# Making the one-hots of an edge-attention kernel on POOL (GpSimd) instead of DVE (VectorE)

## The chip, the cores and the metric

The kernel runs on one core of a Trainium2 chip. Its time is that of one execution on the device, in microseconds; the median of several runs is compared. Engines are named as the profile names them: PE is TensorE's matrix multiplication and PEld its weight load, DVE is VectorE, ACT is ScalarE, POOL is GpSimd and SP is SyncE. POOL here issues the indirect DMAs that gather rows by a list of indices; SP issues the plain loads and stores.

## The reference

One layer of a graph network with attention by edge type: N = 3125 nodes, E = 100000 edges sorted by their destination, R = 5 edge types, 8 heads of 16 channels (H = 128). For every destination and type there is a softmax of its own over the incoming edges.

```python
out = zeros(n, 8, 16)
for r in range(5):
    mask = edge_types == r
    q = einsum('eh,khd->ekd', x[dst], W_Q[r]); k = einsum('eh,khd->ekd', x[src], W_K[r])
    v = einsum('eh,khd->ekd', x[src], W_V[r])
    logits = (q * k).sum(-1) / 4 + attn_bias[r]
    max_v = segment_max(where(mask, logits, -1e9), dst)
    exp_l = where(mask, exp(logits - max_v[dst]), 0)
    attn = exp_l / (segment_sum(exp_l, dst)[dst] + 1e-12)
    out += segment_sum(attn[:, :, None] * v, dst)
out = out.reshape(n, 128) @ out_proj_w.T + out_proj_b
h = layernorm(out + x) * ln_gamma + ln_beta
return layernorm(x + h)
```

## The kernel before

A preparatory phase of about 90 us projects all nodes by all types into a table in HBM, `kv_d` (a row of 256 float32, key and value, for every node and type), and makes `key_d`: for every group of 512 edges the number 5 x (destination - first destination of the group) + type, in bf16. Queries are written, a block of nodes at a time and through the whole run, to `q_d` in three bf16 parts.

Then one loop runs over steps. A group is 512 edges (4 tiles of 128), there are 196 groups, and each step does the *first pass* of one group and the *second pass* of a group 16 to 19 earlier (the maxima of a node must be known before its second pass), 215 steps in all. A block of nodes is finished about every eight steps.

First pass of group g, in the order in which its parts happen:

- `fetch_keys` and `fetch_q` (L365 to L373): SP loads the keys, the same row to all partitions, as `kt` (128 KB, three buffers), and a window of queries as `qw`. This is done three steps ahead.
- `gather` (L678 to L681): POOL issues four indirect DMAs, each of 128 rows of 1 KB, from `kv_d` into one of 21 buffers. A buffer is free when `weigh` of the group 21 earlier is done. Nine groups are gathered before the loop; in the loop a gather is issued two steps ahead.
- `spot` (L735 to L738): the one-hot `hot`, 125 rows by 512 edges in bf16, is 1 where the edge's key is the row's number: one comparison of `kt` with a scalar per partition, `row_of`. It has 21 buffers and is used twice. It is issued two steps ahead, and is the last of the regular instructions of its step on DVE.
- `spread_q` (L740 to L749): PE multiplies the one-hot with the three parts of the queries, 12 matmuls, so that every edge has its query in `qe`. One step ahead.
- `logits` (L756 to L762): DVE multiplies keys and queries (`prod`, L759) and sums by head (L760) into `lg`; SP stores it (L765).

Once per block of nodes, `maxima_load` (L770) collects the block's logits with one indirect DMA on POOL (`ell`, L772), and `maxima` (L779 to L831, DVE) finds the maxima in pieces spread over several steps.

Second pass: `spread_m` (L857, PE) spreads the maxima with the same one-hot, its last use; `less_max` (L872, DVE), `exps` (L876, ACT), `weigh` (L881, DVE: `wv`), `places` (L901 and L904, ACT: `at`), `sums` (L907 to L925, PE: `pp`), `carry` (ACT), `norm` (L936 to L939, DVE: `den`, `o`) and, per block, the projection, the residual and both norms.

The order on each engine is that in which the loop's body is written; no scheduler moves anything. The part that matters here:

```python
        if v is not None:
            weigh(v)
        while gathered < NGR - 1 and step_of[gathered + 1] <= k + AHEAD:   # AHEAD = 2
            gathered += 1
            gather(gathered)
        ...                        # maxima_load, less_max, exps, weights, types, norm
        if g is not None:
            logits(g)
            store_logits(g)
        if k + 2 in group_at:
            spot(group_at[k + 2])
```

Of the kernel before, what the change touches and what calls it, by code (L numbers as in the profile page):

```python
# [12 lines left out]
ALU = mybir.AluOpType  # L13
# [33 lines left out]
WR = WN * R  # L47
# [85 lines left out]
def windowed_path(  # L133
# [4 lines left out]
    nc = tc.nc  # L138
# [90 lines left out]
    def iota(name, pattern, n, base=0, mult=0, dt=F32, pool=const):  # L229
        t = pool.tile([P, n], dt, name=name)  # L230
        nc.gpsimd.iota(
            t, pattern=pattern, base=base, channel_multiplier=mult,
            allow_small_or_imprecise_dtypes=True,
        )
        return t

    node = iota("node", [[P, NT]], NT, mult=1)
    row_of = iota("row_of", [[0, 1]], 1, mult=1)
# [113 lines left out]
    live = {}  # L352
# [381 lines left out]

    def spot(g):  # L735
        hot = hold.tile([WR, T, P], BF16, name="hot")
        nc.vector.tensor_scalar(hot, live.pop(("kt", g))[:WR], row_of[:WR], None, op0=ALU.is_equal)  # L737
        live["hot", g] = hot  # L738

    def spread_q(g):  # L740
# [321 lines left out]
    for k in range(-2, root_at[NT] + 2):  # L1062
        v, g = v_at.get(k), group_at.get(k)
# [59 lines left out]
        if k + 2 in group_at:  # L1123
            spot(group_at[k + 2])
# [535 lines left out]
```

## Time and profile before

| | |
|---|---|
| time, median of 3 runs | 1592.43 us (1591.39 to 1598.67) |
| time of the profiled execution | 1586.14 us |
| its span | 1584.3 us |
| mean granted TensorE clock | 0.714 |
| one-hots on DVE (L737) | 196, 69.2 us busy, 354 ns each |
| gathers on POOL (L681) | 784, 746.9 us busy, 953 ns each |
| maxima loads on POOL (L772) | 25, 23.7 us busy |
| moved by DMA | 203.63 MB |

The profile is of one execution, so sums over its rows are made against 1586.14 us and not against the median. Busy times count only work: the issue of plain DMAs, semaphores and register instructions are left out, but POOL's indirect DMAs are counted, with the time for which POOL is held. In a row of a group, the number behind the bar is busy time in us and the mean of one in ns; then comes the idle time of the engine just before these instructions and what ended most of it.

### The profile page before, as it was taken

How to read it: one execution, taken by the hardware profiler on the slowest of the kernel's cores; microseconds unless marked ns; L12 is line 12 of the kernel's file. 1: busy time of each engine (PE TensorE's matmuls, PEld its weight loads, DVE VectorE, ACT ScalarE, POOL GpSimd, SP SyncE). 2: the span in 40 equal slices, each digit the busy share in tenths (PEclk: the TensorE clock that was granted, in tenths of full speed). 3: DMA queues.
4: the chain of work that ended last, by engine and by line, in shares of the span. 5: the costliest groups of instructions: out<-in, count | busy, mean ns of one | idle time of the engine just before them, and what ended most of it. 6: DMA issues, size and time to landing. Idle time of an engine off the chain costs nothing.

```text
span 1584.3 us, 25675 instructions
## 1 busy us (share of the span) xinstructions
PE 966.0 (61%) x7526; PEld 746.3 (47%) x7526; DVE 928.1 (59%) x2559; ACT 632.1 (40%) x2248; POOL 801.8 (51%) x901
## 2 busy tenths in 40 slices
PE   7940424666666666666556567666666665656775
PEld 3520322545555544545445445454454544545564
DVE  4530722665666466556647646646656665665686
ACT  2630122344444443444434444444444344444354
POOL 2556445445555465455555555555546555555500
PEclk9965556666776687677877777668767677766687
DMA  6963634444554454454554555445445445454400
GB/s 173 362 207 100 149 95 127 118 114 113 137 135 119 127 134 123 116 139 117 129 134 116 134 142 118 120 128 134 121 125 137 123 125 134 115 132 123 115 16 15
DMA packets 180889, 203.63 MB, mean 129 GB/s; under 512 B 83207, under 2 KB 146083, under 8 KB 180620
## 3 DMA queue, kind: packets, MB, share of 16 engines
q0 software_dynamic: 40896, 113.39, 24.8%
q1 hardware_dynamic: 135414, 83.80, 22.9%
q10 hardware_dynamic: 4430, 4.71, 1.1%
q8 instruction: 63, 1.03, 0.3%
q14 instruction: 86, 0.70, 0.1%
HBM read 166.50 MB, written 35.28 MB: 127 GB/s over the span
## 4 chain that ended last, share of the span: by engine, by line
issue 27%; DVE 26%; PE 24%; another core or an unknown queue 7%; ACT 6%; DMA 5%; POOL 3%; SPq 2%; DVEq 0%; ACTq 0%
PE pp L915 8%; DVE prod L759 4%; DVE lg L760 4%; DVE wl L810 4%; DVE wv L881 3%; PE me L863 3%; PE qe L746 3%; PE pr L395 3%; POOL kv L681 3%; DMA mw<-m_d 2%; ACT at L901 2%; DVE mx L816 2%; PE pp L917 2%; DVE hot L737 1%
## 5 line engine op out<-in xcount | busy, mean ns | idle before, releaser
L681 POOL DMA_INDIRECT kv<-kv_d,idx x784 | 746.9, 953 | 602.0 <-DVE den L936 316.4
L915 PE MATMUL pp<-wv,at 128*125 128x136 f32 x1568 | 395.5, 385 | 55.8 <-issue 53.1
L915 PEld LDWEIGHTS pp<-wv,at 128*125 128x125 f32 x1568 | 297.4, 256 | 125.5 <-issue 121.4
L746 PE MATMUL qe<-qw,hot 125*128 125x128 bf16 x2352 | 226.9, 259 | 115.8 <-DVE lg L760 48.6
L863 PE MATMUL me<-mw,hot 125*128 125x64 bf16 (+1 forms) x2352 | 142.2, 218 | 213.7 <-issue 93.0
L746 PEld LDWEIGHTS <-hot 125*128 125x128 bf16 x2352 | 203.5, 126 | 128.7 <-issue 68.7
L876 ACT ACTIVATE me<-me 128x32 f32<-128x32 f32 x196 | 35.7, 182 | 555.9 <-DVE me L872 340.6
L872 DVE TENSOR_TENSOR me<-lg,me 128x32 f32<-128x32 f32 x196 | 37.7, 192 | 373.5 <-remote 170.8
L863 PEld LDWEIGHTS <-hot 125*128 125x128 bf16 x2352 | 125.8, 114 | 249.8 <-issue 213.9
L901 ACT ACTIVATE at<-row_at,nkey 128x125 f32<-128x125 f32 x744 | 237.6, 398 | 0.0
L881 DVE TENSOR_TENSOR wv<-kv,me 128x512 f32<-128x512 f32 x196 | 132.9, 678 | 86.6 <-remote 70.1
L759 DVE TENSOR_TENSOR prod<-kv,qe 128x512 f32<-128x512 f32 x196 | 132.9, 678 | 70.8 <-remote 31.2
L917 PE MATMUL pp<-pt,carried 125*5 125x136 f32 x390 | 100.2, 348 | 63.2 <-ACT pt L930 35.4
L760 DVE TENSOR_REDUCE lg<-prod 128x32 f32<-128x512 f32 x196 | 134.5, 686 | 6.8
L904 ACT ACTIVATE at<-at 128x500 f32<-128x500 f32 (+1 forms) x196 | 117.3, 599 | 6.2
L707 PE MATMUL prq<-wq,xTq 128*128 128x384 f32 (+1 forms) x88 | 51.7, 676 | 108.1 <-DVE hot L737 56.7
L924 PEld LDWEIGHTS pp<-rsum,o 125*128 125x128 f32 x392 | 83.3, 255 | 28.1 <-issue 28.0
L924 PE MATMUL pp<-rsum,o 125*128 125x25 f32 x392 | 74.1, 268 | 24.6 <-issue 20.7
L810 DVE TENSOR_TENSOR wl<-by_head,shut 128x1024 f32<-128x1024 f32 (+2 forms) x73 | 76.9, 1053 | 12.9 <-ACT by_head L787 7.5
L816 DVE TENSOR_REDUCE mx<-wl 128x16 f32<-128x1024 f32 (+2 forms) x73 | 76.5, 1048 | 2.5
L707 PEld LDWEIGHTS prq<-wq,xTq 128*128 128x128 f32 x88 | 19.6, 273 | 116.0 <-DVE hot L737 59.6
L949 ACT COPY oT<-pp 128x25 f32 x196 | 33.2, 169 | 99.1 <-remote 62.3
(184 smaller groups left out, 1024.7 us busy)
## 6 DMA issues: line engine op xcount, KB each, us to landing
kt<-key_d SPq DMA_DIRECT2D x196, 128.0 KB
qw<-q_d SPq DMA_DIRECT2D x196, 96.0 KB
kv_d<-kvs SPq DMA_DIRECT2D x24, 640.0 KB
kv<-kv_d,idx POOLq DMA_INDIRECT x784
q_d<-q SPq DMA_DIRECT2D x22, 480.0 KB
lg_d<-lg SPq DMA_DIRECT2D x196, 18.0 KB
mw<-m_d SPq DMA_DIRECT2D x196, 6.0 KB
xr<-in_x SPq DMA_DIRECT2D x24, 64.0 KB
```

The lines of the kernel that those rows point to most:

```text
L681: nc.gpsimd.indirect_dma_start(out=kv[:, t, :], out_offset=None, in_=kv_d[:, :], in_offset=bass.IndirectOffsetOnAxis(ap=idx[:, t, g : g + ...
L746: nc.tensor.matmul(qe[:, t, :], hot[:, t, :], qw[:WR, s, :], start=(s == 0), stop=(s == 2))
L759: nc.vector.tensor_tensor(prod, kv[:, :, :H], live.pop(("qe", g)), op=ALU.mult)
L760: nc.vector.tensor_reduce(lg[:, :, :HEADS], prod.rearrange("p t (k d) -> p t k d", d=HD), AX.X, ALU.add)
L810: nc.vector.tensor_tensor(wl, by_head[:, None].to_broadcast([P, n, nh, D]), shut[:, :n, None, :].to_broadcast([P, n, nh, D]), op=ALU.add,)
L863: nc.tensor.matmul(me[:, t], hot[:, t, :], mw[:WR, None, :, s, :].to_broadcast([WR, times, 2, HEADS // 2]), start=(s == 0), stop=(s == 2),)
L881: nc.vector.tensor_tensor(wv[:, :, :H].rearrange("p t (k d) -> p t k d", d=HD), kv[:, :, H:].rearrange("p t (k d) -> p t k d", d=HD), live ...
L901: nc.scalar.activation(at[:, t, :], row_at[:, :WR], AF.Abs, bias=nkey[:, t, g : g + 1], scale=1.0)
L904: nc.scalar.activation(at[:, on_dve:], at[:, on_dve:], AF.Relu, bias=1.0, scale=-1.0)
L915: nc.tensor.matmul(pp, at[:, t, :], wv[:, t, :], start=(t == 0), stop=(t == T - 1))
L917: nc.tensor.matmul(pp[:R], carried[:WR, g, :], live.pop(("pt", g - 1)), start=False, stop=False,)
L924: nc.tensor.matmul(op, live.pop(("o5", done)), rsum[:WR], start=True, stop=True)
```

## The change

The comparison that makes the one-hot is issued on POOL instead of DVE, except for the first two groups, which stay on DVE. The call stays where it was in the loop, behind the gathers of the same step, so that on POOL each one-hot stands directly behind the four gathers of its own group (behind the maxima load too, in the steps that have one). The one-hots of groups 2 to 8 stand behind the nine groups gathered ahead of the loop.

```diff
     def spot(g):
         hot = hold.tile([WR, T, P], BF16, name="hot")
-        nc.vector.tensor_scalar(hot, live.pop(("kt", g))[:WR], row_of[:WR], None, op0=ALU.is_equal)
+        on = nc.vector if g < 2 else nc.gpsimd
+        on.tensor_scalar(hot, live.pop(("kt", g))[:WR], row_of[:WR], None, op0=ALU.is_equal)
         live["hot", g] = hot
```

The load of the keys of a later group into the same buffer of `kt` (SP) now waits for POOL instead of DVE, and so does the first weight load of `spread_q` on PE. The orders of instructions on PE, ACT and SP are unchanged.

## The prediction

> **What bounds the kernel now.** I read the busy shares first, then the chain that ended last, the groups, the waits, and windows of the steady loop. All sums are made against the profiled execution (1586.14 us: span 1584.3 and 1.84 outside it); the median of the three timed runs, 1592.43 us, lies 6.3 us above it, and I add that at the end.
>
> Busy shares and the chain:
>
> ```profile
> PE 966.0 (61%) x7526; PEld 746.3 (47%) x7526; DVE 928.1 (59%) x2559; ACT 632.1 (40%) x2248; POOL 801.8 (51%) x901
> issue 27%; DVE 26%; PE 24%; another core or an unknown queue 7%; ACT 6%; DMA 5%; POOL 3%; SPq 2%; DVEq 0%; ACTq 0%
> PE pp L915 8%; DVE prod L759 4%; DVE lg L760 4%; DVE wl L810 4%; DVE wv L881 3%; PE me L863 3%; PE qe L746 3%; PE pr L395 3%; POOL kv L681 3%; DMA mw<-m_d 2%; ACT at L901 2%; DVE mx L816 2%; PE pp L917 2%; DVE hot L737 1%
> ```
>
> No engine is full, and the largest share of the chain, 27%, is "issue": an engine that waited for nothing the profile shows. The one-hot has 1% of the chain. The groups of the change, the engine it leaves and the engine it goes to:
>
> ```profile
> L737 DVE TENSOR_SCALAR hot<-kt,row_of 125x512 bf16<-125x512 bf16 x196 | 69.2, 354 | 4.0 <-DMA kt<-key_d 3.1 <-DMA q_d<-q3s 0.9
> L681 POOL DMA_INDIRECT kv<-kv_d,idx x784 | 746.9, 953 | 602.0 <-DVE den L936 316.4 <-issue 213.1 <-DVE me L872 15.8
> L772 POOL DMA_INDIRECT ell<-lg_d,start_i x25 | 23.7, 949 | 60.4 <-DMA kt<-key_d 24.7 <-DVE me L872 19.1 <-DVE wl L810 7.4
> ```
>
> The waits before a gather, by what ended them (sum in us, count, longest):
>
> ```profile
> POOL kv L681 <- DVE den L936: 316.4, 71, 10.0
> POOL kv L681 <- issue: 213.1, 676, 1.2
> ```
>
> A gather is 0.95 us, and before 676 of the 784 POOL waits for nothing but 213.1 / 676 = 0.3 us of issue, so a group of four holds POOL 4 x (0.95 + 0.30) = 5.0 us. The multiplication `prod` (L759) of group 40 starts at 406.9 us and that of group 190 at 1478.5: 7.14 us per step. With one maxima load of 1.25 us per eight steps POOL needs 5.17 us of a step, and a block of eight steps (57.1 us) has 57.1 - 41.3 = 15.8 us in which POOL waits. The step is thus longer than POOL's 5.17 and than DVE's 4.43 (its busy time of those steps). Where does the rest go? Windows, two of the fill (no pauses between gathers, then no gathers) and two of one steady block:
>
> ```profile
> core 0: us, PE busy (x) PEld busy (x) DVE busy (x) ACT busy (x) POOL busy (x), PEclk, DMA share, GB/s
> 125.00:154.00 29.00, 0.16 (x2) 0.00 (x0) 0.00 (x0) 0.00 (x0) 19.93 (x21) 0.50 0.38 105
> 154.00:177.00 23.00, 13.26 (x113) 10.37 (x113) 17.64 (x34) 2.62 (x11) 0.95 (x1) 0.63 0.50 97
> 755.60:774.30 18.70, 6.88 (x63) 5.09 (x63) 5.51 (x14) 7.67 (x23) 12.33 (x13) 0.75 0.56 161
> 779.20:797.50 18.30, 10.76 (x106) 8.23 (x103) 17.18 (x43) 9.51 (x36) 11.37 (x12) 0.86 0.52 129
> ```
>
> ```profile
> 764.41 0.95 POOL L681 DMA_INDIRECT kv<-kv_d,idx  x1 [0.31 <-issue]
> ...
> 770.68 0.95 POOL L681 DMA_INDIRECT kv<-kv_d,idx  x1 [0.30 <-issue]
> 779.20 0.95 POOL L681 DMA_INDIRECT kv<-kv_d,idx  x1 [7.57 <-DVE den L936]
> ...
> 785.59 0.95 POOL L681 DMA_INDIRECT kv<-kv_d,idx  x1 [1.68 <-DVE den L936]
> ...
> 791.22 0.95 POOL L681 DMA_INDIRECT kv<-kv_d,idx  x1 [0.93 <-issue]
> ```
>
> In 755.6 to 774.3 three groups and a maxima load leave POOL with no pause, and DVE works 5.5 of 18.7 us; in 779.2 to 797.5 three groups with pauses of 1.68 and 0.93 us between them stand beside 17.2 busy us of DVE in 18.3. The fill shows it bare: 29 us of 21 gathers, and PE, DVE and ACT at rest. I counted this over groups 40 to 189: the 51 that start within 0.4 us of the one before have DVE busy 10% of their time, the 62 behind a pause of 0.4 to 3 us 82%, the 37 behind a longer one 85%. I read it so: while gathers run on without a pause, the other engines' instructions crawl. It isn't proved, since the pattern repeats identically in every block: the steps with pauses are those with maxima (much DVE work at hand), and the runs follow quick steps. The readings "runs starve the rest" and "the rest has nothing to do in a run" part at the quick steps.
>
> **The change, part by part.** DVE loses 194 one-hots x 0.354 us = 68.7 us. Most of that lies beside other work: the chain gives `hot` 1%, about 16 us, and this is the gain if nothing else moves. Two one-hots stay on DVE. PE's, ACT's and SP's orders are unchanged.
>
> POOL gains 194 instructions. In its order the nine groups gathered ahead of the loop come first, then the one-hots of groups 2 to 8, then four gathers and a one-hot for each further group (behind the maxima load where there is one).
>
> *Price of a one-hot on POOL.* The trace has no such operation. Nearest are the set-up rows: an iota takes 0.122 us for one element, 0.175 for 64 and 0.233 for 128 (0.9 ns for each further element), and the affine select, which reads and writes 128 elements, 0.293, which over the same 0.12 fixed is 1.35 ns per element. For 512 elements this gives 0.12 + 0.46 = 0.58 us by the iota and 0.12 + 0.69 = 0.81 by the affine select; I take the second, for it has an input. The upper end is twice that, 1.6 us, as a scalar per partition and bf16 are in no POOL row. With 0.30 between instructions h = 1.1 us, ends 0.9 and 1.9.
>
> The Trainium skill ("GPSIMD Engine Reference", elementwise side by side) speaks against this change: it calls GpSimd the wrong engine for ordinary elementwise work, Vector being roughly twice as fast, and its best of about 1.8 cycles per element would make, as an estimate, 0.77 us here. By that page the change is a loss on each instruction; the DVE row of 0.354 agrees with the direction, and whether POOL's idle time pays for it is not a matter the page decides.
>
> *POOL's pace* becomes 5.17 + 1.1 = 6.3 us (6.1 to 7.1) against steps of 7.14. Break-even is h = 1.97.
>
> *A pause in each run.* A group now has 1.1 us without a gather behind it, as long as the pauses of 0.93 to 1.68 beside which DVE was 82% busy. If these end the crawl, the quick steps (2.9 us of DVE work) proceed under the gathers and POOL sets the pace: a block is 8 x (5.0 + 1.1) + 1.25 = 50.1 us. I leave it 1.3 us of waits for buffers (the 21 buffers even out the blocks' long steps of 5.6 to 6.4 us), so 51.4 against 57.1: 5.7 less, over 165 steps or 20.6 blocks, 117 us. With h = 0.9 a block is 49.8 (150 us less), with h = 1.6 it is 55.4 (35 less), with 1.9 some 57.8: nothing gained.
>
> *New waits.* A one-hot on POOL waits for its keys (`kt`) and for its buffer of 21 (freed by PE's `spread_m`). Behind it stand all later gathers. Keys are loaded three steps ahead, 128 KB, and the 4.0 us of idle before L737 are the only trace of them being late, so I take nothing. SP's load of the next keys now waits for POOL, and behind that stand SP's other loads and the stores of logits; as POOL stands a step ahead, nothing is late. PE's `spread_q` needs the one-hot one step later, but it is queued behind four gathers. In the profile `spread_q` starts on average 2.64 us after the gathers of its group end, yet in about a quarter of the steps up to 1.6 us before it. Those steps would wait: some 0.6 us per step on average if the pace were unchanged. In the likely case a faster PE waits for POOL anyway, and this is in the pace.
>
> *The fill.* Today the first run of gathers lasts to 151 us; it will end at 136, when the one-hots wait for keys. PE, DVE and SP start up to 15 us earlier, and the gathers of 9 to 20 come at 6.1 us each instead: I take half, 7 us.
>
> The sum: 1586 - 117 - 7 = 1462 on the profiled execution, and 1468 on the median. As h has more room above 1.1 than below, and 1.3 us of waits a block is sparing (now it is 15.8), I put the likeliest at 1485, with 1430 to 1565 as its own range (h of 0.9, and h of 1.7 with 16 us from DVE).
>
> **The rivals.** (1) *The rest still crawls and POOL is only longer* (slower). If the stall is not ended by a one-hot behind a group, or comes from the order of the work and not from the gathers, then POOL's 15.8 us of waits per block stay and 8 x 1.1 = 8.8 us are added: 20.6 x 8.8 = 181 us, 1773 on the median. If only the quarter of the steps in which `spread_q` waits for the one-hot is paid, it is 0.6 x 165 = 100 us: 1692. For it: cause and occasion coincide in every block, and POOL waits mostly for `den`, the end of `weigh` of a slow step. Against it: the pauses of 0.93 us did suffice. It decides once h plus the waits that stay go above 1.97 us a step. (2) *Hidden and worth nothing*: POOL's 15.8 idle us a block take the 8.8, and the 68.7 us of DVE were not on the path: 1592, or 1576 with the chain's 16 us. That the change does not do what it says is no rival: the two built programs differ by these 194 instructions and the waits that go with them, and by nothing else.
>
> **How the numbers follow.** Likely case 0.55, the slower rival 0.35, the neutral one 0.10. A measurement of this kernel tells about 0.5% (8 us) from no change; half of the neutral case falls within that, the other half, with the chain's 16 us, is faster, and of the likely case 0.01 ends within 0.5% (h near 1.9). Faster 0.59, same 0.06, slower 0.35. The range runs from 1430 (h = 0.9) to 1690 (the waits of `spread_q` paid in full), which leaves out some 0.05 below and 0.15 above. The likeliest case alone would be 1430 to 1565.
>
> **What would show it.** Right: a POOL one-hot of 0.6 to 1.1 us, no stretch of 10 us with DVE under 30%, POOL over 80% busy with its gaps, "issue" well below 27% of the chain, idle time of L681 behind `den` falling from 316 to under 100 us. Wrong: one-hots of over 1.6 us, PE rows of L746 that wait for `hot` on POOL, or windows behind the one-hot in which DVE is still at rest; then the crawl isn't ended by a pause of this length, or wasn't made by the runs.

## The result, and the profile after

The changed kernel took 1506.32 us (median of 4 runs, 1504.7 to 1506.73) beside 1593.89 us for the kernel before in the same comparison: a ratio of 0.9445, 95% interval 0.9421 to 0.947. Its profiled execution took 1506.07 us, with a span of 1504.3, against 1586.14 and 1584.3 before. The prediction said 1485 in 1430 to 1690. As the experiments show further down, the sign of this result goes with the chip it ran on: on another chip the same change made the kernel 21% slower.

The page of the changed kernel: busy shares, the two lines of the chain that ended last, and three groups (busy us, mean ns, then idle before and what ended most of it):

```profile
PE 1005.8 (67%) x7526; PEld 800.1 (53%) x7526; DVE 901.7 (60%) x2365; ACT 637.9 (42%) x2248; POOL 1123.9 (75%) x1095
POOL 36%; PE 26%; issue 15%; DVE 11%; DMA 7%; another core or an unknown queue 2%; SPq 1%; ACT 1%; DVEq 0%; POOLq 0%; ACTq 0%
POOL kv L681 22%; POOL hot L738 14%; PE qe L747 6%; PE pp L916 6%; PE me L864 5%; DMA kv<-kv_d,idx 5%; PE pr L395 3%; DVE lg L761 2%; DVE prod L760 1%; PE prq L707 1%; PE pp L918 1%; PE pp L925 1%; DMA mw<-m_d 1%; POOL ell L773 1%
L681 POOL DMA_INDIRECT kv<-kv_d,idx x784 | 761.4, 971 | 227.6 <-issue 172.0
L747 PE MATMUL qe<-qw,hot 125*128 125x128 bf16 x2352 | 248.9, 283 | 435.1 <-POOL hot L738 393.1
L738 POOL TENSOR_SCALAR hot<-kt,row_of 125x512 bf16<-125x512 bf16 x194 | 308.9, 1592 | 14.3 <-DMA kt<-key_d 8.4
```

The wait of the gathers for `den` (316.4 us) is gone from L681, "issue" has fallen from 27% to 15% of the chain, and POOL has taken the chain over. The one-hot lasts 1.59 us. POOL's timeline shows a group in the steady loop (start, duration, idle before):

```profile
736.38 0.95 POOL L681 DMA_INDIRECT kv<-kv_d,idx  x1 [0.30 <-DMA kv<-kv_d,idx]
737.37 1.58 POOL L738 TENSOR_SCALAR hot<-kt,row_of 125x512 bf16<-125x512 bf16 x1
739.12 1.00 POOL L681 DMA_INDIRECT kv<-kv_d,idx  x1 [0.17 <-issue]
740.43 0.98 POOL L681 DMA_INDIRECT kv<-kv_d,idx  x1 [0.31 <-issue]
```

Nothing but issue stands between POOL's instructions: 0.30 us between gathers, 0.03 ahead of the one-hot and 0.17 behind it. So a step needs 4 x 0.971 + 3 x 0.30 + 0.03 + 1.592 + 0.17 us, and 0.16 for an eighth of a maxima load: 6.74 us. From `prod` of group 40 (377.9 us) to that of group 190 (1391.6) a step takes 6.76. POOL sets the pace to 0.3%, and over these steps no idle stretch of POOL is longer than 0.4 us. Windows of the changed kernel, in the fill and over eight steps of the loop:

```profile
core 0: us, PE busy (x) PEld busy (x) DVE busy (x) ACT busy (x) POOL busy (x), PEclk, DMA share, GB/s
125.00:135.00 10.00, 0.00 (x0) 0.00 (x0) 0.00 (x0) 0.00 (x0) 7.56 (x9) 0.50 0.39 114
699.59:752.32 52.73, 36.73 (x288) 30.00 (x288) 33.17 (x88) 24.96 (x88) 43.75 (x40) 0.69 0.53 133
```

DVE works 63% of the eight steps. In the fill it is still at rest. A new wait lies there as well: SP's load of the sixth group's keys needs the one-hot of the third, which stands on POOL behind nine groups of gathers. In this trace it delays nothing, since SP itself reaches that load only at 145.6 us and the one-hot is done at 140.1. In the changed kernel's run on another chip, further down, SP was through with what stands ahead of that load at 106.6 us and issued it at 136.05, when the one-hot was done.

Where the 80.0 us of the span went, by `prod`: up to group 40, 29.0 us (406.9 to 377.9), of which only 3.9 by group 20; from 40 to 190, 57.8 (1071.5 to 1013.7); behind 190, 6.9 us were lost (105.8 to 112.7). Between groups 20 and 40 a step fell from 8.0 us to 6.73.

### The profile page after: what moved, and what is told of

It reads as the page before. It is cut to its first block, busy times and chain, and to the rows that moved or that the text cites. A ratio compares the mean times of both kernels' runs of the same rounds, so it can differ in the third digit from the quotient of the medians.

```text
span 1504.3 us, 26147 instructions
## 1 busy us (share of the span) xinstructions
PE 1005.8 (67%) x7526; PEld 800.1 (53%) x7526; DVE 901.7 (60%) x2365; ACT 637.9 (42%) x2248; POOL 1123.9 (75%) x1095
## 4 chain that ended last, share of the span: by engine, by line
POOL 36%; PE 26%; issue 15%; DVE 11%; DMA 7%; another core or an unknown queue 2%; SPq 1%; ACT 1%; DVEq 0%; POOLq 0%; ACTq 0%
POOL kv L681 22%; POOL hot L738 14%; PE qe L747 6%; PE pp L916 6%; PE me L864 5%; DMA kv<-kv_d,idx 5%; PE pr L395 3%; DVE lg L761 2%; DVE prod L760 1%; PE prq L707 1%; PE pp L918 1%; PE pp L925 1%; DMA mw<-m_d 1%; POOL ell L773 1%
## 5 line engine op out<-in xcount | busy, mean ns | idle before, releaser
L681 POOL DMA_INDIRECT kv<-kv_d,idx x784 | 761.4, 971 | 227.6 <-issue 172.0
L747 PE MATMUL qe<-qw,hot 125*128 125x128 bf16 x2352 | 248.9, 283 | 435.1 <-POOL hot L738 393.1
L747 PEld LDWEIGHTS <-hot 125*128 125x128 bf16 x2352 | 202.8, 130 | 461.1 <-POOL hot L738 424.1
L916 PE MATMUL pp<-wv,at 128*125 128x136 f32 x1568 | 407.1, 402 | 0.0
L916 PEld LDWEIGHTS pp<-wv,at 128*125 128x125 f32 x1568 | 312.3, 272 | 69.4 <-issue 69.1
L738 POOL TENSOR_SCALAR hot<-kt,row_of 125x512 bf16<-125x512 bf16 x194 | 308.9, 1592 | 14.3 <-DMA kt<-key_d 8.4
L864 PE MATMUL me<-mw,hot 125*128 125x64 bf16 (+1 forms) x2352 | 149.3, 229 | 24.9 <-DMA mw<-m_d 14.9
L864 PEld LDWEIGHTS <-hot 125*128 125x128 bf16 x2352 | 137.0, 123 | 51.5 <-issue 36.5
L395 PE MATMUL pr<-wkv,xT 128*128 128x512 f32 x150 | 60.8, 547 | 3.6 <-issue 3.1
```

Source lines behind the costliest of these rows:

```text
L681: nc.gpsimd.indirect_dma_start(out=kv[:, t, :], out_offset=None, in_=kv_d[:, :], in_offset=bass.IndirectOffsetOnAxis(ap=idx[:, t, g : g + ...
L738: on.tensor_scalar(hot, live.pop(("kt", g))[:WR], row_of[:WR], None, op0=ALU.is_equal)
L747: nc.tensor.matmul(qe[:, t, :], hot[:, t, :], qw[:WR, s, :], start=(s == 0), stop=(s == 2))
L864: nc.tensor.matmul(me[:, t], hot[:, t, :], mw[:WR, None, :, s, :].to_broadcast([WR, times, 2, HEADS // 2]), start=(s == 0), stop=(s == 2),)
L916: nc.tensor.matmul(pp, at[:, t, :], wv[:, t, :], start=(t == 0), stop=(t == T - 1))
```

## The experiments

The theory (A): gathers that follow each other without a pause slow the other engines, a pause ends that, and POOL then sets the pace. The rival (B): the gain is the work taken off DVE.

**Pause alone.** The kernel before, with an unread comparison on POOL behind every group from the third on.

```diff
     def spot(g):
         ...
         nc.vector.tensor_scalar(hot, live.pop(("kt", g))[:WR], row_of[:WR], None, op0=ALU.is_equal)
+        if g >= 2:
+            nc.gpsimd.tensor_scalar(idle_out, idle_in, row_of[:WR], None, op0=ALU.is_equal)
```

> The one-hots stay on DVE as before; POOL runs a comparison of the same size on a constant tile of its own behind every group from the third on, whose output nobody reads. So POOL has the same pause and the same load as in the changed kernel (1592 ns per comparison), and DVE is not relieved. Theory A (a pause behind each group lets the other engines work, and POOL then sets the pace of 6.7 us per step): about the changed kernel's 1506 us, 1495 to 1530. Theory B (the gain comes from the 68.7 us of work taken off DVE): no gain, POOL's added work is lost or hidden, 1590 to 1700.

Measured 1498.24 us; the kernel before took 1643.74 in this comparison, so the ratio is 0.9108 (0.9066 to 0.915). Steps of groups 40 to 190 take 6.760 us, the changed kernel's 6.758. Its groups on POOL:

```profile
L685 POOL DMA_INDIRECT kv<-kv_d,idx x784 | 763.4, 974 | 227.9 <-issue 193.5
L743 POOL TENSOR_SCALAR idle_out<-idle_in,row_of 125x512 bf16<-125x512 bf16 x194 | 308.0, 1588 | 6.6
```

POOL carries the same load as in the changed kernel for an output that nobody reads, DVE keeps its one-hots, and the pace is the same. So the gain needs the pause and not the relief of DVE: A holds on this point, and B adds nothing to it. Whether the gathers slow the others, or these have no work in a run of gathers, is not settled by this run.

**DVE relief alone.**

```diff
     ...                                     # prod: one tile, set to zero ahead of the loop
-        nc.vector.tensor_tensor(prod, kv[:, :, :H], live.pop(("qe", g)), op=ALU.mult)
+        qe, h = live.pop(("qe", g)), T // 2
+        nc.vector.tensor_tensor(prod[:, :h], kv[:, :h, :H], qe[:, :h], op=ALU.mult)
```

> The one-hots stay on DVE, and POOL does nothing new; the multiplication of keys and queries is made for half of each group's edges only (the other half's logits are zero), which takes some 0.32 us per group off DVE, 63 us in all, about what the one-hots took. Theory A: the crawl under unbroken gathers is as before, so little is gained: 1565 to 1594. Theory B: about the changed kernel's time, 1500 to 1530.

This kernel leaves out the logits of half the edges. Measured 1622.76 us, ratio 0.9871 (0.9803 to 0.994) on the same chip: 21 us for the 53 taken off (`prod` lasts 0.410 us a group instead of 0.678; 63 in all had been expected). That is near the 16 us that the chain's 1% allowed, and far from the pause's 145.

**Shorter pauses.** Half of each one-hot on POOL, and then an unread comparison of 128 elements.

```diff
-        nc.vector.tensor_scalar(hot, live.pop(("kt", g))[:WR], row_of[:WR], None, op0=ALU.is_equal)
+        kt, d = live.pop(("kt", g))[:WR], T if g < 2 else ON_DVE      # ON_DVE = 2
+        nc.vector.tensor_scalar(hot[:, :d], kt[:, :d], row_of[:WR], None, op0=ALU.is_equal)
+        if d < T:
+            nc.gpsimd.tensor_scalar(hot[:, d:], kt[:, d:], row_of[:WR], None, op0=ALU.is_equal)
```

> Half of each one-hot (two of four tiles) is made on DVE and half on POOL, from the third group on. Theory A: the POOL comparison of 256 elements lasts about 0.85 us (half of 1592 ns and a fixed part), so POOL needs some 0.75 us less per step: 168 x 0.75 = 125 us less than 1506, 1370 to 1400, if no other engine takes over the pace; a pause of 0.85 us is close to the shortest pauses (0.93 us) of the kernel before, so a time near 1450 would say that a shorter pause ends the crawl only in part. Theory B: between the two kernels, 1530 to 1560.

> As the run with the pause alone, but the unread comparison on POOL has 128 elements instead of 512: some 0.45 us. One-hots on DVE. Theory A with POOL as the only bound: POOL needs 5.5 us per step, 1.2 us less than in the changed kernel, 200 us less than 1506, down to 1310; with another bound in between 1350 to 1450. Theory A with a pause that has to have a certain length: back towards 1594. Theory B: 1590 to 1620.

Measured 1501.02 us (ratio 0.9153, 0.9095 to 0.9211) and 1539.46 (0.9377, 0.9327 to 0.9427). Both miss the expected gain. The groups of the first on POOL:

```profile
L681 POOL DMA_INDIRECT kv<-kv_d,idx x784 | 761.1, 971 | 327.3 <-issue 190.8 <-DVE den L941 87.0 <-DMA kv_d<-kvs 13.6
L742 POOL TENSOR_SCALAR hot<-kt,row_of 125x256 bf16<-125x256 bf16 x194 | 187.2, 965 | 19.6 <-DMA kt<-key_d 13.5
```

POOL needs 6.11 us of a step here (the sum above with 0.965 in place of 1.592), the step takes 6.71, and the waits for `den` are back. With 128 elements (0.636 us) it needs 5.78 and the step takes 6.94. POOL is asked for less here, and waits for the others again. The three sizes give a price of about 0.32 us and 2.5 ns for each element.

**The changed kernel again, long runs, short runs.** This set ran on another chip.

```diff
+        if g >= 2 and g % 2:                        # long runs: two behind every second group
+            for _ in range(2):
+                nc.gpsimd.tensor_scalar(idle_out, idle_in, row_of[:WR], None, op0=ALU.is_equal)
...
+            if g >= 9 and t % 2 == 1:               # in gather(g): 128 elements behind every two;
+                nc.gpsimd.tensor_scalar(            # the last one: 32 behind every gather
+                    idle_out[:, :128], idle_in[:, :128], row_of[:WR], None, op0=ALU.is_equal
+                )
```

> The changed kernel again, beside the runs of this call, since the kernel before took 3% longer in the first comparison of experiments than in the prediction's. If POOL's 6.74 us per step set its pace, its time does not follow what slowed the kernel before: 1495 to 1515.

> As the run with the pause alone (one-hots on DVE, an unread comparison of 512 elements on POOL), but two comparisons stand together behind every second group: runs of eight gathers (10 us) and pauses of 3.3 us, with the same load on POOL. Theory A1 (the crawl begins some 5 us into an unbroken run of gathers, so the length of the runs counts): slower than with one pause per group, 1530 to 1600. Theory A2 (only the share of pauses counts, or the even pace of POOL): as with one pause per group, 1495 to 1510.

> One-hots on DVE; an unread comparison of 128 elements on POOL behind every two gathers, from the tenth group on: 635 ns each by the run with the short pause, so POOL needs 4 x 0.97 + 2 x (0.30 + 0.03 + 0.64 + 0.17) + 0.16 = 6.3 us per step. Theory A1: runs of two gathers never crawl, POOL sets the pace, 6.3 us, 0.4 us below the changed kernel's 6.76: about 1430 to 1450. Theory A2: as the run with half of the one-hot on POOL, whose pauses take nearly the same time, 1490 to 1510.

> One-hots on DVE; an unread comparison of 32 elements on POOL behind every gather, from the tenth group on: some 0.39 us each by the line through the three sizes measured (0.31 us and 2.45 ns per element), so POOL needs about 6.5 us per step. Theory A1: the shortest runs possible, POOL sets the pace: 1440 to 1480. If a pause needs a certain length to help, the gathers count as one run again: 1540 to 1600. Theory A2: 1490 to 1510.

Measured 1503.27, 1503.08, 1417.14 and 1457.84 us. But the kernel before took 1242.33 us on this chip (7 runs, 1237.75 to 1244.47), and the changed kernel's ratio is 1.2115 (1.2085 to 1.2146). The changed kernel's time had hardly moved. All four were slower than the kernel before, with steps (groups 40 to 190) of 6.80, 6.83, 6.41 and 6.63 us that POOL's work sets; between A1 and A2 this set could not decide, since there was little here for a pause to cure.

**The kernel before, profiled on a further chip.** No edit; beside it the kernel with a pause behind every two gathers.

> The kernel before once more, for its profile on another chip: it took 1594, 1644 and 1242 us in three comparisons, the changed kernel 1506 and 1503. Theory C (chips differ in how far gathers without a pause slow the other engines; where they do not, POOL's 5.17 us per step sets the pace): near 1242 the profile shows steps of about 5.2 us, POOL without waits, and DVE at work in the long runs of gathers; near 1600 it shows the runs with DVE at rest, as in the prediction's profile. Theory D (the difference lies outside the loop, such as the preparatory phase or the clock): the steps are 7.1 us in any case.

> The kernel with a pause behind every two gathers again (one-hots on DVE). On a chip where the kernel before takes some 1600 us: theory A1 (short runs do not slow the others) 1410 to 1440, as on the chip where the kernel before took 1242, since POOL sets the pace; if the slowing depends on the share of pauses only, 1490 to 1510, as with half of the one-hot on POOL. On a chip where the kernel before takes some 1240 us: 1417 again.

The kernel before took 1240.07 us, the other 1418.23 (1.1413, 1.1388 to 1.1438). The profile of the kernel before on this chip (busy shares, the gathers, and windows of the fill and of the loop):

```profile
PE 855.1 (69%) x7526; PEld 671.3 (54%) x7526; DVE 932.3 (75%) x2559; ACT 632.6 (51%) x2248; POOL 799.0 (65%) x901
L681 POOL DMA_INDIRECT kv<-kv_d,idx x784 | 743.9, 949 | 308.6 <-issue 195.9
```

```profile
core 0: us, PE busy (x) PEld busy (x) DVE busy (x) ACT busy (x) POOL busy (x), PEclk, DMA share, GB/s
125.00:135.00 10.00, 3.84 (x20) 2.40 (x18) 3.73 (x7) 1.09 (x3) 7.56 (x9) 0.50 0.57 155
135.00:145.00 10.00, 4.90 (x38) 3.77 (x36) 4.69 (x9) 1.17 (x6) 7.56 (x9) 0.50 0.57 148
494.19:582.47 88.28, 60.48 (x608) 49.15 (x609) 70.55 (x194) 50.10 (x179) 62.51 (x66) 0.83 0.68 166
```

The kernel before on the chip of the prediction, in the same stretch of the fill:

```profile
125.00:135.00 10.00, 0.16 (x2) 0.00 (x0) 0.00 (x0) 0.00 (x0) 7.59 (x8) 0.50 0.47 120
135.00:145.00 10.00, 0.00 (x0) 0.00 (x0) 0.00 (x0) 0.00 (x0) 7.59 (x8) 0.50 0.36 105
```

The same program, the same run of gathers (7.6 us busy on POOL in each 10); on one chip the others rest, on the other DVE works 37 to 47% of the stretch. The granted clock is 0.50 in all four rows, and the DMA engines are less busy where the others rest (0.36 to 0.47 against 0.57), so neither the clock nor full DMA engines account for it. Counted as for the prediction: of groups 40 to 189 here 120 start within 0.4 us of the one before, and beside these DVE is busy 80% of the time (10% on the first chip). The step is 5.54 us. So D falls, and C holds in the main: the step is not quite the 5.2 us of POOL's need, as the gathers still wait 64.5 us for `den` here, against 316.4. It also settles what the prediction left open: a run of gathers does not lack work for the others, since in the same order of work they work beside it on this chip.

A row of the traces shows the crawl by itself. Ahead of each load of queries SP moves a register (L373). Its 196 moves (shortest, median and longest in ns), in the kernel before on the first chip and on this one:

```profile
L373 SPq MOVE qw<-q_d x196: 3/29/705, 92.5 to 1485.9; - x196
L373 SPq MOVE qw<-q_d x196: 29/29/38, 90.9 to 1144.0; - x196
```

On the first chip 68 of the moves take more than 100 ns, and 65 of these begin while gathers follow each other without a pause. So there the instructions themselves are slow, and not only short of data. The longest move is 700 ns or more in all seven profiles from comparisons in which the kernel before takes 1594 to 1644 us, and 38 ns in all seven from the others. The kernels with a pause are no exception: 700 ns in the changed kernel, 721 with the pause alone. So their pauses do not end the slowing; they keep it from setting the pace.

**All pauses in one execution.** Seven parts of 24 groups with different pauses, twice.

```diff
+    def pause(part, g, t):
+        if part == 1 and t % 2:
+            idle(128)
+        if part == 2:
+            nc.gpsimd.memset(one, 0.0)
+        if part == 3 and t == T - 1:                # in the second kernel only
+            idle(256)
+        if part == 4 and t == T - 1 and g % 2:
+            idle(512)
+            idle(512)
+        if part == 5 and t == T - 1:
+            idle(512)
+        if part == 6:
+            idle(32)
...
+            pause((g - 20) // 24, g, t)             # in gather(g), behind each of the four
```

> One-hots on DVE throughout; in seven parts of 24 groups (from group 20 on) POOL's pauses differ, so that they are compared in one execution on one chip, by the mean time per group over the last 16 groups of each part. Part 0 and 3: none. Part 1: 128 elements behind every two gathers (POOL needs 6.4 us per group, as measured). Part 2: a memset of one element behind every gather (POOL needs 4 x (0.95 + 0.03 + 0.09 + 0.17) + 0.16 = 5.1 us). Part 4: twice 512 elements behind every second group (6.8). Part 5: 512 elements behind every group (6.76). Part 6: 32 elements behind every gather (6.6). On a chip where the kernel before takes some 1600 us, parts 0 and 3 take 7.1 to 7.4. Theory A1 (the length of unbroken runs counts): part 1 6.4, part 6 6.6, part 5 6.76, part 4 over 7.0; part 2 near 5.5 if any instruction between gathers ends the slowing, 7.1 or more if POOL has to be free of gathers for a time. Theory A2 (the share of pauses counts): parts 1, 4, 5 and 6 all at POOL's need or 6.7 to 6.8. On a chip where it takes 1240 us: parts 0, 2 and 3 5.5, the others at POOL's need.

> As the kernel in parts before it (part 0 no pause; 1: 128 elements behind every two gathers; 2: a memset of one element behind every gather; 4: twice 512 elements behind every second group; 5: 512 behind every group; 6: 32 behind every gather), with part 3 now 256 elements behind every group, since that kernel ran on a chip where the kernel before takes 1240 us and its parts only followed POOL's need (5.2, 6.4, 5.6, 6.8, 6.7, 6.7). On a chip where the kernel before takes some 1600 us: part 0 7.4; theory A1 (length of runs): part 1 6.4, part 3 6.7 as with half of the one-hot on POOL, part 4 over 7.0, part 5 6.76, part 6 6.75, part 2 near 5.6 if any instruction in between ends the slowing, 7.1 or more if not. Theory A2 (share of pauses): part 1 about 6.7, like part 3, and part 4 6.8 like part 5. On a chip where it takes 1240 us: part 3 some 6.1, POOL's need, and the others as before.

The first ran where the kernel before takes 1239.86 us (1349.45, ratio 1.0868, 1.0787 to 1.095), the second where it takes 1603.88 (1535.14, ratio 0.9595, 0.9487 to 0.9703). Windows over the last 16 groups of each part, in order, first kernel and then second; a length divided by 16 is the time per group:

```profile
core 0: us, PE busy (x) PEld busy (x) DVE busy (x) ACT busy (x) POOL busy (x), PEclk, DMA share, GB/s
231.74:315.57 83.83, 61.35 (x570) 49.90 (x570) 67.92 (x187) 45.75 (x161) 62.81 (x67) 0.78 0.68 175
367.10:469.77 102.67, 70.54 (x599) 57.13 (x597) 71.77 (x194) 49.91 (x178) 85.65 (x99) 0.71 0.57 142
514.40:604.13 89.73, 61.78 (x618) 50.17 (x616) 71.56 (x197) 50.87 (x180) 70.00 (x130) 0.83 0.66 163
648.33:737.49 89.16, 59.72 (x594) 47.79 (x594) 70.55 (x193) 50.00 (x178) 62.39 (x67) 0.85 0.66 164
793.18:902.50 109.32, 71.99 (x591) 57.85 (x590) 73.09 (x190) 50.31 (x178) 89.32 (x82) 0.71 0.52 133
956.46:1064.33 107.87, 70.96 (x596) 56.82 (x596) 73.38 (x194) 50.61 (x180) 89.35 (x82) 0.72 0.53 134
1117.32:1225.31 107.99, 70.59 (x605) 57.72 (x602) 72.82 (x190) 49.25 (x175) 94.02 (x132) 0.69 0.51 132
```

```profile
core 0: us, PE busy (x) PEld busy (x) DVE busy (x) ACT busy (x) POOL busy (x), PEclk, DMA share, GB/s
296.49:414.36 117.87, 75.23 (x585) 60.03 (x585) 71.33 (x195) 50.43 (x179) 62.51 (x66) 0.69 0.50 129
465.86:568.37 102.51, 66.86 (x580) 53.75 (x578) 71.50 (x194) 50.43 (x180) 85.50 (x99) 0.75 0.57 143
623.33:743.89 120.56, 75.73 (x594) 60.08 (x594) 70.85 (x194) 49.84 (x178) 70.11 (x130) 0.69 0.47 121
797.38:906.13 108.75, 72.57 (x595) 56.58 (x595) 71.43 (x195) 50.39 (x179) 79.19 (x83) 0.70 0.54 135
963.06:1074.34 111.28, 72.53 (x588) 57.12 (x585) 69.84 (x192) 48.70 (x176) 88.42 (x82) 0.70 0.53 129
1129.26:1237.22 107.96, 68.74 (x589) 55.81 (x588) 74.08 (x194) 50.53 (x179) 89.42 (x82) 0.73 0.54 137
1290.72:1398.88 108.16, 67.06 (x594) 54.16 (x593) 71.37 (x190) 49.19 (x175) 94.24 (x132) 0.72 0.51 131
```

| pause on POOL | chip of 1240 us, us per group | chip of 1604 us, us per group |
|---|---|---|
| none (part 0) | 5.24 | 7.37 |
| 1 element behind each gather (2) | 5.61 | 7.54 |
| 256 elements behind each group (3) | (none in the first kernel: 5.57) | 6.80 |
| 128 elements behind every two gathers (1) | 6.42 | 6.41 |
| 512 elements behind each group (5) | 6.74 | 6.75 |
| 32 elements behind each gather (6) | 6.75 | 6.76 |
| twice 512 behind every second group (4) | 6.83 | 6.96 |

DVE does the same work in every row (68 to 74 us). Where POOL's need is 6.4 us or more, the two chips agree within 0.02 us in three rows and part by 0.13 in the fourth; where it asks less, they part by far more. A one-element memset cures nothing (7.54 beside 7.37): the gathers then follow each other as fast as without (0.03 + 0.12 + 0.17 us instead of 0.30). A pause behind every two gathers does as A1 said (6.41), better than a single one of 256 elements (6.80). Against A1, runs of eight gathers with long pauses are only 0.13 us worse than on the other chip and stay below its 7.0; against A2, part 1 is not at 6.7. Neither theory is confirmed in full. At the same amount of pause, one behind each group against two behind every second (6.75 and 6.96), the spacing counts for 0.2 us, less than A1 had it. Parts 1 and 3 differ in spacing and in amount (2 x 0.64 us of comparisons per group against 0.95), so how much of 6.41 against 6.80 is due to the spacing is not shown.

## Why the prediction was right, and where it was off

*Sign and mechanism.* The pause mechanism was the likeliest case, and on a chip where the kernel before is as slow as in the prediction's profile, or slower, it is what happened: the pause alone gives the whole pace, DVE's relief alone 1.3%. It works in another way than the prediction said, though: the crawl is not ended, as SP's moves show, but no longer holds up POOL. The count by pauses (10% against 82%) pointed the right way, and the confounder that the prediction named was settled by the kernel before on another chip. The forecast had no term for the chip; its sign came out because the comparison ran where the kernel before takes 1594 us and not 1240, and that much was luck.

*The price of the one-hot* was the mis-sized term: 0.81 us taken, 1.592 measured, just inside the upper end of 1.6 for the instruction. The slope of the affine select (1.35 ns per element) was carried to a comparison with a scalar per partition in bf16, which costs 2.5 ns. What the Trainium skill's "GPSIMD Engine Reference" (elementwise side by side) makes of it as an estimate, 0.77 us, is as far off. That Vector is "roughly 2×" faster, which its opening says and the same section measures for a float32 addition, is 1592 / 354 = 4.5 here. As the one-hot replaces one gap of 0.30 by 0.20 us, the addition per step is 1.49 us, not 1.1; with gathers of 0.971 for 0.953 it is 1.56.

*The waits that stay* (1.3 us a block) were none: POOL never waits in the loop. Together the steady part fell by 57.8 us over 150 steps where the sum had 107 (5.7 / 8 x 150). That the whole came nearer is in part luck: the 20 steps from group 20 to 40 gave 25.1 us where the sum's rate gives 14, and the likeliest value had been put 17 us above the sum as a margin.

*The new waits.* PE did wait for the one-hot (sum in us, count, longest):

```profile
PEld L747 <- POOL hot L738: 424.1, 191, 6.7
```

It cost nothing beyond POOL's pace, as said. The prediction also named such waits among its signs of being wrong; where POOL sets the pace they are no such sign. Keys were late by 8.4 us in all, ahead of group 40. That confirms "nothing" for the loop. In the fill, 7 us gained were 3.9 by group 20. There SP's load of keys, which the prediction had behind a POOL that "stands a step ahead", is behind nine groups; in the changed kernel's run on the other chip that held SP for 29 us.

*The marks.* POOL's share, "issue" and the wait for `den` came as told; the one-hot's length did not, nor the mark that no 10 us pass with DVE under 30% busy: about 1% of such stretches of the loop do (lowest 27%), against 13% before.

*The slower rival* was weighed on the wrong ground. Its mechanism, POOL longer with nothing in return, is real: where the gathers don't slow the others, a step goes from 5.54 to 6.8 us, and the kernel from 1242 to 1503. The prediction asked whether the slowing existed, and not whether it exists on every chip.

## What to carry to other kernels

When "issue" and idle engines pile up beside long unbroken runs on one engine, change only the spacing of that engine's instructions first: an unread instruction there costs a line and separates a pause from the work that is moved. A change whose gain rests on such an interference is to be measured on several chips, since kernels that POOL's work paces (the changed kernel 1506 and 1503 us in two comparisons, the pause alone 1498 in a third) and one that the interference paces (1240 to 1644) trade places. Where the kernel must serve both, a pause behind every two gathers costs less than one as long as the moved one-hot (6.41 against 6.75 us per group on both; the whole kernel with it, 1417 us, was timed only where the kernel before takes 1240), though none of the versions tried beats the kernel before where it takes 1240 us.

## What the runs showed of the hardware

- Indirect gathers on POOL with 0.30 us between them slow the instructions of PE, DVE, ACT and SP on some chips and not on others: the kernel before took 1594, 1644 and 1604 us in three comparisons, and 1242, 1241 and 1240 in three more (the last two on one chip), each steady within 1%. The gathers themselves last the same (953 and 949 ns). Why the chips differ was not found, nor whether it is the chip itself or something else that stayed the same throughout a comparison; nothing was tried that changes the gathers themselves (larger ones, another table layout).
- A register move on SP tells the two apart in any profile here: its longest is 700 ns or more on the first kind, 38 ns on the second.
- The slowing no longer sets the pace where POOL issues two gathers and then does 0.63 us of something else (6.41 us per group on both kinds), and a memset of 0.12 us behind each gather does not help (7.54 us).
- A comparison with a scalar per partition, 125 x 512 in bf16, takes POOL 1592 ns and DVE 354.
